# Graph quantile layer: 56 list gathers of the last pair as one-hot products on TensorE, and products and one-hot rows of the last batches on ACT

## The chip, the cores and the metric

The kernel runs on one core of a Trainium2 chip. The metric is device time in microseconds of one launch. Three runs of the kernel before gave 1544.91, 1548.63 and 1550.77 us; their median, 1548.63 us, is the time before. In this text PE is TensorE (PEld its weight load), DVE is VectorE, ACT is ScalarE, POOL is GpSimd and SP is SyncE. A tile is held as 128 partitions by some elements; a size such as 128x384 gives both.

## The reference

There are 16 graphs ("batches") of 1024 nodes with 64 channels each. The neighbours of a node are thinned by a rule on their rank; of each channel's values over the node and its remaining neighbours the quartiles are taken and added with weights 1/4, 1/2, 1/4; the sum goes through two dense layers. Cut to what matters:

```python
h = relu(layernorm(x))                                   # 16 x 1024 x 64
neigh = (adj > 0) & ~eye
nb = neigh.sum(-1);  rank = cumsum(neigh) - neigh
skip = where(nb > 10, (nb + 1) // 2, 1)
rem = neigh & (skip > 1) & (rank % skip == skip - 1) & mask
rem = rem | rem.T
nd = (adj > 0 or eye) and not rem                        # who counts for node n
s = sort(where(nd, h, inf), axis=neighbours);  nv = nd.sum()
for tau, w in ((.25, .25), (.5, .5), (.75, .25)):
    pos = tau * (nv - 1)
    agg += w * (s[floor(pos)] + frac(pos) * (s[ceil(pos)] - s[floor(pos)]))
out = x + (relu((h + agg) @ W1 + b1) @ W2 + b2) * mask
```

## The kernel before

The kernel has a list path, list_layer, which does all the work on this data, and a dense path behind a flag, which isn't entered here.

**Stages.** Batches go in pairs (m = 0 to 7, batches 2m and 2m+1). For each batch, prepare (L1629) loads the adjacency matrix, thins it (drop, keep), orders the 1024 nodes by their number of neighbours (order) and makes for each node a list of its neighbours' row numbers (collect, which ends with idx at L1132; lists[b] holds it). normalize writes the normalized rows of the batch to a table in DRAM. Then fetch (L1253) gathers, for each pair, the neighbours' rows of 64 f32 values: one indirect DMA of POOL (L1265) for each batch h, node tile k and list place s moves 128 rows. Nodes are ordered by list length, so the eight tiles of 128 nodes have lists of different lengths: FULL and HOSTS (L78, L79) set 12, 10, 9, 8, 8, 7, 5 and 4 gathers for tiles 0 to 7, 63 for each batch and 126 for a pair; the node's own row comes from an ACT copy (L1262). Eight pairs make the 1008 gathers of L1265. The 32 nodes with the longest lists are treated apart, for eight batches at a time ("the group", tile gg, with gathers of its own at L1531).

**Classes.** Tiles are sorted in four classes, (0), (1, 2, 3), (4, 5) and (6, 7), with 13, 11, 9 and 7 slots. The tile of a class is g0, g1, g4 or g6, with two buffers for g0 and g1 and one for g4 and g6 (bufs=2 - lo // 4): the next pair's gathers of tiles 4 to 7 wait until this pair has left them. sort (L1278) runs a fixed network of min and max over the slots of a class (L1297, L1300, L1305, on DVE), then multiplies the slots that can hold a quantile by their coefficients (L1316, on DVE, up to 384 elements an instruction) and lets PE add them into PSUM with an identity matrix (L1320). The order in which the slots are filled is in PLANS.

**Output.** After a pair's sums, ACT splits them into three bf16 terms (L1333), one_hot (L1414) makes rows that compare a running index with each node's number (L1418, DVE), and PE brings the sums back to the nodes' own order with them (sums, L1434 and L1440) and runs the two layers (mlp, L1448). For pairs 0 to 6 this follows the pair's sums; for the last pair the two halves and the two batches are interleaved by hand (aggregate with between, L1350 and L1650), so that batch 14's layers run beside batch 15's sort.

**Order.** The program is written as generators that yield costs. weave (L1602) runs results(m - 1) (sums and layers of the pair before) and beside it, in proportion, prepare for the next pair; and it issues the queued gathers bit by bit. In the loop at L1678, m = 7 has no batches left to prepare, so results(6) runs there with no side work, while the gathers of pair 7 are issued; m = 8 runs results(7). Afterwards arrange (L641) takes all instructions, works out who needs what, and sets each engine's order: it walks through time with costs of its own (cost, L614: 1330 ns for a gather, 55 ns + 0.87 ns an element and 75 ns a column operand for ACT, PE at its full clock) and at each moment gives an engine the ready instruction that stands first in the program. The engines then run in that fixed order. So a change in one place moves instructions elsewhere too. opened (L796) puts a very short memset (L799) behind a DVE instruction, and settle (L779) keeps a run of matmuls together with one semaphore at its end.

Of the kernel before, what the change touches and what calls it, by code (L numbers as in the profile page):

```python
# [31 lines left out]
F32 = mybir.dt.float32  # L32
F16 = mybir.dt.float16
BF16 = mybir.dt.bfloat16
# [30 lines left out]
CLASSES = (((0,), 13), ((1, 2, 3), 11), ((4, 5), 9), ((6, 7), 7))  # L65
# [19 lines left out]
FRONT = 134  # L85
# [667 lines left out]
def list_layer(  # L753
# [490 lines left out]
    def issue(many=None):  # L1244

        while queue and (many is None or many > 0):
# [3 lines left out]
            turn[0] += 1  # L1250
            many = None if many is None else many - 1

    def fetch(m, classes=CLASSES, halves=(0, 1)):  # L1253

        for tiles, slots in classes:
            lo, n = tiles[0], len(tiles)
            held, order = PLANS[slots][:2]

            def begin(h, tiles=tiles, lo=lo, n=n, slots=slots, held=held):
                if (m, tiles) not in gathered:  # L1260
                    gathered[m, tiles] = wk.tile([P, held, n, 2, C], F32, name=f"g{lo}", bufs=2 - lo // 4)
                nc.scalar.copy(gathered[m, tiles][:, slots - 1, :, h], owns[m][:, lo:lo + n, h])  # L1262

            def gather(h, slot, k, at, tiles=tiles, lo=lo):
                return nc.gpsimd.indirect_dma_start(  # L1265
                    out=gathered[m, tiles][:, slot, k - lo, h], out_offset=None, in_=tables[2 * m + h][0],
                    in_offset=bass.IndirectOffsetOnAxis(ap=lists[2 * m + h][:, at:at + 1], axis=0),
                    element_offset=tables[2 * m + h][1],
                )

            for h in halves:
                queue.append(partial(begin, h))
                for k in tiles:
                    for s, slot in enumerate(order[:FULL[k] + ((k, FULL[k]) in HOSTS)]):
                        queue.append(partial(gather, h, slot, k, PASSED[k] + s))


    def sort(lines, plan, first, coef, acc):  # L1278

        size = prod(lines.shape[2:])  # L1280

        def at(first, step, n):
            stop = first + step * (n - 1) + (1 if step >= 0 else -1)
            return lines[:, first:stop if stop >= 0 else None:step or 1]

        _, _, steps, ends, taken = plan
        most = max(1, PART // size)

        def parts(n):
            return [(k, min(most, n - k)) for k in range(0, n, most)]  # L1290

        for n, a, da, b, db, f, df, back, what in steps:
            run, others = [], []
# [13 lines left out]
            loose.update((then.ins.name, ins.ins.name) for ins, then in zip(run, others))  # L1307
            cost = (0.16 + n * size / 960) * (1 if f < 0 else 2)
            yield cost
        for n in taken:  # L1310
            now, ends = ends[:n], ends[n:]
            for k, many in parts(n):
                some = now[k:k + many]
                v = at(some[0], some[1] - some[0] if many > 1 else 0, many)
                v = v.rearrange("p s (k c) -> p s k c", c=C) if len(lines.shape) == 3 else v
                opened(nc.vector.tensor_tensor(  # L1316
                    v, v, coef(first + k, many)[:, :, :, None].to_broadcast(list(v.shape)), OP.mult
                ))
            settle([
                nc.tensor.matmul(  # L1320
                    acc, ident32, lines[:, s], start=False, stop=(s == now[-1] and not ends), skip_group_check=True
                )
                for s in now
            ])
            first += n
            cost = 0.16 + n * size / 960
            yield cost
# [22 lines left out]
    def aggregate(m, o, between=None):  # L1350
# [4 lines left out]
        for half in (0, 1) if last else (1, 0):  # L1355
            parts = CLASSES[2 * half:2 * half + 2][::1 if last else -1]
            for sides in ((0, 1), (1, 2)) if last and half else ((0, 2),):
# [56 lines left out]
    def one_hot(b, n, tag="at_p", bufs=1):  # L1414

        at = wk.tile([P, NT, HALF], BF16, name="at_p", tag=tag, bufs=bufs)
        for t in range(NT):
            opened(nc.vector.tensor_scalar(  # L1418
                at[:, t], iota[:, n * HALF:(n + 1) * HALF], node[:, b, t:t + 1], None, OP.is_equal
            ))  # L1420
            if t % 2:
                yield 0.6
        placed[b, n] = at
# [178 lines left out]
    def weave(main, total, side, side_total):  # L1602

        done = spent = 0.0
        turn[0] = 0
        for cost in main:
            done += cost / total
            issue(max(0, int(done * SPREAD) - turn[0]))
            while side is not None and spent / side_total < done:
                got = next(side, None)  # L1610
                if got is None:
                    side = None
                else:
                    spent += got
        for _ in side or ():
            pass
        issue()
# [89 lines left out]
def window(tiles, n):  # L1707

    return min(LEAST[k] for k in tiles) // 4, -(-3 * (n - 1) // 4) + 1
# [165 lines left out]
```

## Time and profile before

| | |
|---|---|
| Median of the runs | 1548.63 us |
| The profiled execution | 1547.62 us |
| Its span, first to last instruction | 1545.8 us |
| Mean granted PE clock | 0.840 |
| Last list ready (L1132, batch 15) | 1237.7 us |
| Last gather of pair 6 issued | about 1297 us |
| Last gather of pair 7 issued | 1487.5 us |
| Last sorting step | 1524.1 us |

"Busy" is the time in which an engine executes an instruction. An engine that isn't busy waits for data, for a buffer, or for its own issue. A group row gives the line, engine, operation and tiles, the count, the busy time in all and the mean of one in ns, then the idle time of the engine just before them and what ended it. A row of waits gives who waited for whom: us in total, how often, the longest. Matmuls of f32 count twice in the counts[...]. Instructions of DVE and ACT overlap their neighbours by a little, so the distance between two starts is shorter than the duration of one.

### The profile page before, as it was taken

What the parts mean: (1) busy time and instruction counts of PE and PEld (TensorE: products, weight loads), DVE (VectorE), ACT (ScalarE), POOL (GpSimd) and SP (SyncE); (2) the same over time, 40 slices, a digit from 0 to 9 for tenths busy, and PEclk for the clock granted to TensorE, in tenths of its full rate; (3) what the DMA queues carried; (4) which work ended last, traced back from release to release, by engine and by line L of the source; (5) the groups of instructions that cost most, each with busy time, mean ns of one, the idle gap of its engine ahead of it and who ended that gap; (6) DMA issues with size and microseconds to landing.
All of it is one profiled execution on the core that took longest, in us unless ns stands there. A gap on an engine that the chain in (4) does not pass through costs nothing.

```text
span 1545.8 us, 28097 instructions
## 1 busy us (share of the span) xinstructions
PE 1067.7 (69%) x8411; PEld 663.0 (43%) x8411; DVE 1249.8 (81%) x6125; ACT 915.4 (59%) x2504; POOL 1110.3 (72%) x1051
## 2 busy tenths in 40 slices
PE   6777867889886986798829964459867942450256
PEld 3444544555564544455516543335534521220223
DVE  5625389985899889978996798988998899689784
ACT  6998976989877884789557682186834410110001
POOL 3177775777777777777777777777777777777760
PEclk9979869899998998899869996769977975685567
DMA  6353432434433343335322342232311121121100
GB/s 213 103 178 87 118 93 78 114 86 122 96 111 86 88 126 83 87 76 129 85 66 79 67 133 50 45 100 59 93 34 28 26 53 24 30 52 24 25 15 16
DMA packets 128532, 122.85 MB, mean 79 GB/s; under 512 B 94546, under 2 KB 95090, under 8 KB 128370
## 3 DMA queue, kind: packets, MB, share of 16 engines
q1 hardware_dynamic: 95026, 86.77, 18.6%
q0 software_dynamic: 33344, 34.19, 12.0%
q8 instruction: 68, 1.11, 0.3%
q14 instruction: 94, 0.77, 0.2%
HBM read 110.10 MB, written 9.05 MB: 77 GB/s over the span
## 4 chain that ended last, share of the span: by engine, by line
ACT 28%; PE 23%; issue 18%; POOL 14%; DVE 10%; DMA 6%; DVEq 0%; SPq 0%; ACTq 0%; POOLq 0%
POOL g L1265 13%; PE codeP L1088 6%; ACT dist L991 5%; PE acc L1320 5%; ACT sg L904 4%; ACT ne L924 3%; ACT kept L1014 3%; DVE g L1300 2%; ACT waste L1186 2%; DMA at<-in_adj_dram 2%; DMA g<-gtab,idx 2%; DVE g L1305 2%; ACT waste L1181 2%; ACT xt L1194 2%; PE rk L981 1%
## 5 line engine op out<-in xcount | busy, mean ns | idle before, releaser
L1265 POOL DMA_INDIRECT g<-gtab,idx x1008 | 1055.0, 1047 | 367.7 <-issue 288.6
L1305 DVE TENSOR_TENSOR g<-g 128x384 f32<-128x384 f32 (+2 forms) x675 | 310.7, 481 | 6.4 <-DMA gg<-g 6.1
L1300 DVE TENSOR_TENSOR g<-g 128x384 f32<-128x384 f32 (+2 forms) x675 | 313.2, 484 | 1.5
L1320 PE MATMUL acc<-g,kf 128*128 128x128 f32 (+2 forms) x472 | 141.0, 448 | 159.9 <-DVE g L1316 106.6
L1088 PE MATMUL codeP<-pack,perm 128*128 128x332 bf16 x1024 | 184.9, 321 | 14.9 <-DVE perm L1063 14.5
L991 ACT ACTIVATE dist<-rk,bias 128x512 f16<-128x512 f32 x256 | 168.5, 708 | 31.2 <-DVE rem L992 19.9
L981 PE MATMUL rk<-kb,cnt 128*128 128x512 bf16 x256 | 112.5, 440 | 91.4 <-ACT dist L991 85.5
L1320 PEld LDWEIGHTS acc<-g,kf 128*128 128x128 f32 x472 | 90.1, 232 | 188.5 <-DVE g L1316 110.6
L911 PE MATMUL tp<-kb,sg 128*128 128x128 bf16 x1024 | 108.2, 242 | 71.6 <-ACT sg L904 50.2
L1014 ACT ACTIVATE kept<-kp 128x512 fp8e4<-128x512 f32 x248 | 146.8, 615 | 11.3 <-PE kp L1009 9.3
L924 ACT ACTIVATE ne<-tp 128x512 fp8e4<-128x512 f32 x248 | 141.5, 622 | 17.1 <-PE tp L917 9.7
L986 PEld LDWEIGHTS <-ne 128*128 128x128 fp8e4 x1024 | 89.9, 109 | 143.8 <-issue 120.9
L799 DVE MEMSET pause<- 128x1 bf16 x2340 | 138.1, 59 | 0.0
L904 ACT ACTIVATE sg<-at 128x1024 bf16<-128x1024 f32 x121 | 128.7, 1086 | 5.2 <-DMA at<-in_adj_dram 5.2
L1088 PEld LDWEIGHTS <-perm 128*128 128x128 bf16 x1024 | 93.4, 101 | 78.2 <-DVE perm L1063 37.8
L911 PEld LDWEIGHTS <-sg 128*128 128x128 bf16 x1024 | 80.6, 109 | 95.3 <-ACT sg L904 56.0
L986 PE MATMUL rk<-kw,ne 128*128 128x128 fp8e5 x1024 | 118.3, 241 | 0.0
L992 DVE TENSOR_SCALAR rem<-dist,half 128x1024 bf16<-128x1024 f16 x128 | 64.2, 503 | 52.2 <-ACT dist L991 51.4
L1009 PE MATMUL kp<-kw,rem 128*128 128x128 fp8e5 x1024 | 99.4, 218 | 0.0
L1004 PE MATMUL kp<-ne,kw 128*128 128x512 fp8e4 x256 | 97.2, 380 | 0.4 <-ACT dist L991 0.2
L1005 PE MATMUL kp<-rem,kw 128*128 128x512 bf16 x256 | 96.5, 377 | 0.0
L1418 DVE TENSOR_SCALAR at_p<-iota,node 128x512 bf16<-128x512 f16 x256 | 85.6, 376 | 11.8 <-PE low L1440 11.8
(189 smaller groups left out, 2071.5 us busy)
## 6 DMA issues: line engine op xcount, KB each, us to landing
at<-in_adj_dram SPq DMA_DIRECT2D x122, 512.0 KB
g<-gtab,idx POOLq DMA_INDIRECT x1008
xt<-in_x_dram SPq DMA_DIRECT2D x16, 256.0 KB
y<-in_x_dram SPq DMA_DIRECT2D x16, 256.0 KB
gtab<-xt SPq DMA_DIRECT2D x16, 256.0 KB
out_dram<-y SPq DMA_DIRECT2D x14, 256.0 KB
spare<-in_adj_dram SPq DMA_DIRECT2D x6, 512.0 KB
gg<-g SPq DMA_DIRECT2D x32, 48.0 KB
```

The costliest lines, as they stand in the source:

```text
L799: tails[nc.vector.memset(pause[:, at:at + 1], 0.0).ins.name] = ins.ins.name
L904: nc.scalar.activation(sg, at, AF.Sign)
L911: run.append(nc.tensor.matmul(tp[:, s], sg[:, m * P:(m + 1) * P], ident16, start=(s == 0), stop=(s == 3 and t // 4 != n), skip_group_check ...
L924: nc.scalar.activation(to, tp, AF.Relu, saturate=False)
L986: run.append(nc.tensor.matmul(rk[:, s * P:(s + 1) * P], ne[:, 4 * n + s, ts], upper, start=False, stop=(s == 3), skip_group_check=True,))
L991: nc.scalar.activation(dist[:, n * HALF:(n + 1) * HALF], rk, AF.Abs, bias=bias[:, t:t + 1])
L1014: nc.scalar.activation(kept[:, 4 * n:4 * n + 4], kp, AF.Relu, saturate=False)
L1088: run.append(nc.tensor.matmul(flat, perm[:, t, k * P:(k + 1) * P], pack[:, t], start=False, stop=(t == NT - 1), skip_group_check=True,))
L1265: return nc.gpsimd.indirect_dma_start(out=gathered[m, tiles][:, slot, k - lo, h], out_offset=None, in_=tables[2 * m + h][0], in_offset=bas ...
L1300: nc.vector.tensor_tensor(at(f + k * df, df, many), pa, pb, OP.min if what == "<" else OP.max)
L1305: nc.vector.tensor_tensor(pa if back else pb, pa, pb, OP.max if what == "<" else OP.min)
L1320: nc.tensor.matmul(acc, ident32, lines[:, s], start=False, stop=(s == now[-1] and not ends), skip_group_check=True)
```

## The change

Three things change, all in the last two pairs.

1. **Picks.** Of pair 7's gathers, the first LEAST[k] places of each list (LEAST = 8, 4, 4, 4, 4, 4, 0, 0 for tiles 0 to 7) are no longer issued to POOL: 28 for each batch, 56 in all. New functions do them. begin_pick reads the rows of batches 14 and 15 back from the table in DRAM, and splits each f32 into a bf16 half and two bytes in bf16 (three terms of 64 columns, exact). pick goes through the 56 in seven lots of eight. For each place, PE multiplies the broadcast index column by an identity matrix, so that the 128 row numbers stand along the free dimension on every partition; ACT copies them to f16 ("rows"); DVE compares them with the node number of each partition, for each of eight blocks of 128 nodes ("hot", 128x1024 an instruction, one buffer, in the place called "wide"); PE multiplies the one-hot blocks by the terms, 8 products of 192 columns a pick; ACT writes the result into the class tile, the bf16 half and the two bytes.
2. **Products on ACT.** For pairs 6 and 7 (ACTP = 6) the products by coefficients are done by ACT, one instruction of 64 elements with a scale column for each slot, tile and batch.
3. **One-hot rows on ACT.** For batches 14 and 15 (ACTB = 14) one_hot uses two ACT instructions for each DVE instruction: |index - node|, then relu(1 - that).

At m = 7 the picks are the side work of the weave: 20 steps of them are put ahead of results(6), the rest woven through it.

```diff
+ACTP, ACTB = 6, 14
...
+    def opening(some, m=B // 2 - 1):
+
+        tiles, slots = some
+        if (m, tiles) not in gathered:
+            gathered[m, tiles] = wk.tile(
+                [P, PLANS[slots][0], len(tiles), 2, C], F32, name=f"g{tiles[0]}", bufs=2 - tiles[0] // 4
+            )
...
                     for s, slot in enumerate(order[:FULL[k] + ((k, FULL[k]) in HOSTS)]):
-                        queue.append(partial(gather, h, slot, k, PASSED[k] + s))
+                        if m < pairs - 1 or s >= LEAST[k]:
+                            queue.append(partial(gather, h, slot, k, PASSED[k] + s))
+
+    def begin_pick():
...
+        nc.vector.tensor_scalar(first, first, float(FRONT), None, OP.add)
...
+            nc.sync.dma_start(
+                out=xt, in_=tab[at // C + FRONT:at // C + FRONT + N].rearrange("(t p) c -> p t c", p=P)
+            )
+            t = wk.tile([P, NT, 3 * C], BF16, name="terms", tag="at", bufs=2)
...
+            nc.scalar.copy(t[:, :, :C], halves[:, :, :, 1])
+            nc.scalar.copy(t[:, :, C:].rearrange("p t (c k) -> p t c k", k=2), bytes_[:, :, :, 0:2])
...
+    def pick(first, terms, index, wanted):
+
+        m = pairs - 1
+        for n in range(0, len(wanted), 8):
+            some = wanted[n:n + 8]
+            rows = wk.tile([P, len(some), P], F16, name="rows", tag="dist", bufs=2)
+            for at in range(0, len(some), 4):
+                tp = psum.tile([P, 4, P], F32, name="rowsT", tag="mx", bufs=3)
+                settle([
+                    nc.tensor.matmul(
+                        tp[:, q], index[h][:, PASSED[k] + s:PASSED[k] + s + 1].to_broadcast([P, P]), ident32,
+                        start=(q == 0), stop=(q == 3), skip_group_check=True,
+                    )
+                    for q, (h, k, s) in enumerate(some[at:at + 4])
+                ])
+                nc.scalar.copy(rows[:, at:at + 4], tp)
+            yield 0.5
+            hot = wk.tile([P, NT, 8, P], BF16, name="hot", tag="wide", bufs=1)
+            for j in range(NT):
+                opened(nc.vector.tensor_scalar(hot[:, j, :len(some)], rows, first[:, j:j + 1], None, OP.is_equal))
+                if j % 2:
+                    yield 1.0
+            for at in range(0, len(some), 2):
+                (h, k, s), (h2, k2, s2) = some[at:at + 2]
...
+                got = psum.tile([P, 2, 3 * C], F32, name="got", tag="code", bufs=2)
+                settle([
+                    nc.tensor.matmul(
+                        got[:, q], hot[:, j, at + q], terms[h][:, j], start=(j == 0 and q == 0),
+                        stop=(j == NT - 1 and q == 1), skip_group_check=True,
+                    )
+                    for q in range(2) for j in range(NT)
+                ])
...
+                nc.scalar.copy(halves[:, :, :, 1], got[:, :, :C])
+                nc.scalar.copy(bytes_[:, :, :, 0:2], got[:, :, C:].rearrange("p s (c k) -> p s c k", k=2))
+                yield 1.0
...
-    def sort(lines, plan, first, coef, acc):
+    def sort(lines, plan, first, coef, acc, by_act=False):
...
+                if by_act:
+                    w = coef(first + k, many)
+                    for i in range(many):
+                        for j in range(v.shape[2]):
+                            nc.scalar.activation(v[:, i, j], v[:, i, j], AF.Copy, scale=w[:, i, j:j + 1])
+                    continue
...
                         lines, plan, window(tiles, slots)[0], weigh, acc[:, lo - 4 * half:lo - 4 * half + n],
+                        m >= ACTP,
                     )
...
+            if b >= ACTB:
+                nc.scalar.activation(
+                    at[:, t], iota[:, n * HALF:(n + 1) * HALF], AF.Abs, bias=node[:, b, t:t + 1], scale=-1.0
+                )
+                nc.scalar.activation(at[:, t], at[:, t], AF.Relu, bias=ones_r[:, 0:1], scale=-1.0)
+            else:
+                opened(nc.vector.tensor_scalar(
+                    at[:, t], iota[:, n * HALF:(n + 1) * HALF], node[:, b, t:t + 1], None, OP.is_equal
+                ))
...
-        weave(chain(results(m - 1) if m else (), (1.0,)), 140.0 if m else 1.0, side, 85.0)
+        if m == pairs - 1:
+            side = pick(*begin_pick(), [
+                (h, k, s) for tiles, _ in CLASSES[:3] for h in range(2) for k in tiles for s in range(LEAST[k])
+            ])
+            for _ in range(20):
+                next(side)
+        weave(chain(results(m - 1) if m else (), (1.0,)), 140.0 if m else 1.0, side, 85.0 if m < pairs - 1 else 45.0)
```

More of the change, by code (lines that the diff above doesn't have):

```diff
@@ L1259, in begin @@
             def begin(h, tiles=tiles, lo=lo, n=n, slots=slots, held=held):
-                if (m, tiles) not in gathered:
-                    gathered[m, tiles] = wk.tile([P, held, n, 2, C], F32, name=f"g{lo}", bufs=2 - lo // 4)
+                opening((tiles, slots), m)
                 nc.scalar.copy(gathered[m, tiles][:, slots - 1, :, h], owns[m][:, lo:lo + n, h])
@@ L1274, in fetch @@
                     for s, slot in enumerate(order[:FULL[k] + ((k, FULL[k]) in HOSTS)]):
-                        queue.append(partial(gather, h, slot, k, PASSED[k] + s))
-    def sort(lines, plan, first, coef, acc):
+                        if m < pairs - 1 or s >= LEAST[k]:
+                            queue.append(partial(gather, h, slot, k, PASSED[k] + s))
+    def begin_pick():
+        first = wk.tile([P, NT], F32, name="first", bufs=1)
+        nc.vector.tensor_tensor(first, own2.rearrange("p (t k) -> p t k", k=2)[:, :, 0], own2.rearrange("p (t k) -> p t k", k=2)[:, :, 1], OP.add)
+        nc.vector.tensor_scalar(first, first, float(FRONT), None, OP.add)
+        terms, index = [], []
+        for h in range(2):
+            b = 2 * (pairs - 1) + h
+            xt = wk.tile([P, NT, C], F32, name="xt", bufs=1)
+            tab, at = tables[b]
+            nc.sync.dma_start(
+                out=xt, in_=tab[at // C + FRONT:at // C + FRONT + N].rearrange("(t p) c -> p t c", p=P)
+            )
+            t = wk.tile([P, NT, 3 * C], BF16, name="terms", tag="at", bufs=2)
+            halves, bytes_ = (
+                xt.rearrange("p t c -> p (t c)").bitcast(d).rearrange("p (t c k) -> p t c k", t=NT, c=C)
+                for d in (BF16, U8)
+            )
+            nc.scalar.copy(t[:, :, :C], halves[:, :, :, 1])
+            nc.scalar.copy(t[:, :, C:].rearrange("p t (c k) -> p t c k", k=2), bytes_[:, :, :, 0:2])
+            terms.append(t)
+            f = wk.tile([P, PASSED[-1]], F32, name="index", tag="keys", bufs=2)
+            nc.scalar.copy(f, lists[b])
+            index.append(f)
+        return first, terms, index
@@ new lines, in pick @@
+    def pick(first, terms, index, wanted):
[21 more added lines that the diff above has]
+                (h, k, s), (h2, k2, s2) = some[at:at + 2]
+                tiles, slots = next(c for c in CLASSES if k in c[0])
+                to = PLANS[slots][1][s:s + 2]
+                got = psum.tile([P, 2, 3 * C], F32, name="got", tag="code", bufs=2)
[6 more added lines that the diff above has]
+                ])
+                opening((tiles, slots))
+                step = to[1] - to[0]
+                end = to[1] + (1 if step > 0 else -1)
+                line = gathered[m, tiles][:, to[0]:end if end >= 0 else None:step, k - tiles[0], h]
+                halves, bytes_ = (line.bitcast(d).rearrange("p s (c k) -> p s c k", c=C) for d in (BF16, U8))
+                nc.scalar.copy(halves[:, :, :, 1], got[:, :, :C])
+                nc.scalar.copy(bytes_[:, :, :, 0:2], got[:, :, C:].rearrange("p s (c k) -> p s c k", k=2))
+                yield 1.0
@@ L1417, in one_hot @@
         for t in range(NT):
-            opened(nc.vector.tensor_scalar(
-                at[:, t], iota[:, n * HALF:(n + 1) * HALF], node[:, b, t:t + 1], None, OP.is_equal
-            ))
+            if b >= ACTB:
+                nc.scalar.activation(
+                    at[:, t], iota[:, n * HALF:(n + 1) * HALF], AF.Abs, bias=node[:, b, t:t + 1], scale=-1.0
+                )
+                nc.scalar.activation(at[:, t], at[:, t], AF.Relu, bias=ones_r[:, 0:1], scale=-1.0)
[3 more added lines that the diff above has]
+                ))
             if t % 2:
```

## The prediction

> **What bounds the kernel now.** I read four views in this order: the page's busy shares and chain, the waits of POOL and DVE after 1236 us, busy time by stretch there, and the rows of the operations that the change touches. 1236 us is where the last batch's lists are finished (idx, L1132, last at 1237.7 us); nothing that the change adds for batch 15 can start sooner.
>
> ```profile
> PE 1067.7 (69%) x8411; PEld 663.0 (43%) x8411; DVE 1249.8 (81%) x6125; ACT 915.4 (59%) x2504; POOL 1110.3 (72%) x1051
> L1265 POOL DMA_INDIRECT g<-gtab,idx x1008 | 1055.0, 1047 | 367.7 <-issue 288.6
> ```
>
> POOL looks less busy than DVE, but each gather of 1047 ns is followed by some 0.3 us of issue gap: 72% busy is a queue without a hole.
>
> ```profile
> POOL g L1265 <- issue: 50.3, 165, 0.3
> POOL g L1265 <- DMA g<-gtab,idx: 1.5, 5, 0.3
> ```
>
> These are POOL's waits from 1236 us on: no stall longer than 1.5 us until the last gather at 1487.5 us. So POOL is saturated to 58 us before the end. But DVE in the same stretches (columns: us, PE, PEld, DVE, ACT, POOL busy, PE clock, DMA share, GB/s):
>
> ```profile
> 1236.00:1256.00 20.00, 17.05 (x80) 8.91 (x78) 18.67 (x108) 6.61 (x17) 15.19 (x16) 1.00 0.27 53
> 1256.00:1337.00 81.00, 12.31 (x36) 7.65 (x37) 80.51 (x391) 0.59 (x2) 63.33 (x59) 0.55 0.17 33
> 1337.00:1376.00 39.00, 33.67 (x153) 19.18 (x152) 21.72 (x113) 12.02 (x24) 29.86 (x31) 0.93 0.21 46
> 1376.00:1433.00 57.00, 4.50 (x18) 4.12 (x19) 56.20 (x251) 0.00 (x0) 44.50 (x42) 0.50 0.15 29
> 1433.00:1444.00 11.00, 9.01 (x49) 7.92 (x47) 0.62 (x4) 1.27 (x4) 8.26 (x10) 0.78 0.15 26
> 1444.00:1524.00 80.00, 32.99 (x138) 18.30 (x138) 72.31 (x350) 7.49 (x19) 44.30 (x34) 0.67 0.10 18
> 1524.00:1546.00 22.00, 12.79 (x52) 7.15 (x52) 4.22 (x12) 3.67 (x7) 0.00 (x0) 0.66 0.06 16
> sum 310.00, PE 122.32 PEld 73.22 DVE 254.25 ACT 31.64 POOL 205.44; mean PE 17.47 PEld 10.46 DVE 36.32 ACT 4.52 POOL 29.35
> ```
>
> DVE is busy for 254.3 of these 310 us. Its idle time, stretch by stretch, is 1.3, 0.5, 17.3, 0.8, 10.4, 7.7 and 17.8 us. ACT is all but empty: 31.6 us of 310. What DVE waits for there:
>
> ```profile
> DVE yp L1508 <- PE yp L1504: 14.9, 6, 10.3
> DVE at_p L1418 <- PE low L1440: 7.1, 4, 5.7
> DVE highs L1461 <- PE low L1440: 7.0, 1, 7.0
> DVE g L1378 <- PE acc L1320: 6.6, 2, 3.7
> ```
>
> No line names a gather. The waits are the output layers of pair 6 and of the group, which the written-out order put where it had no sorting that it held ready. Gathers decide DVE's idle time only in this indirect way, through the order. So from 1236 us on there are two bounds close together, and DVE's is the harder: 254 us of work, of which the change takes little.
>
> **What the Trainium skill says.** *Perfetto Trace Analysis*, § Identifying the Most-Contended Engine: for Vector, Scalar and GPSIMD, occupancy is a fair measure of nearness to the limit. For DVE the trace agrees (80.51 of 81 us); for POOL it misleads, since the 0.3 us gaps are not counted. *VectorE: DVE Perf Modes*, § The perf-mode tier table: a tensor_scalar on 16-bit data in SBUF runs at 4x, an fp32 tensor_tensor at 1x. The trace agrees: 1024 16-bit elements take 478 ns at L1063, 384 fp32 ones 550 ns at L1305. *SBUF — State Buffer*, § Who interferes with whom: a DVE op in a two-port mode keeps GpSimd out of the shared ports. Gathers take 0.94 us where DVE idles (1433 to 1444 us) and 1.13 to 1.25 beside sorting; the added one-hot comparisons are of the locking kind. *ScalarE: Activation LUTs*, § What ACT_TABLE_LOAD costs: each [128,1] pointer operand adds about 93 ns and neighbours overlap by as much. L1186 (one pointer, 64 elements) takes 348 ns against 260 for L1181 without one, and its successor starts 0.25 us after it.
>
> **The change, part by part.**
>
> *Gathers removed.* Tiles 0 to 5 give up LEAST = 8, 4, 4, 4, 4, 4 slots in each of two batches: 56 of pair 7's 126. From 1349.5 to 1487.5 us POOL issues 102 gathers, 1.35 us each, so 56 are worth 76 us of POOL: its last gather would move from 1487.5 to about 1412 us. Pair 6's last 44 gathers, to 1297 us, remain.
>
> *One-hot rows added to DVE.* 56 picks in 7 lots of 8; each lot is 8 comparisons of 128x1024 f16 into bf16. Shape, types and operation are those of L1063, whose starts lie 0.41 us apart: 56 x 0.41 = 23 us. Bound: 27 us if nothing overlaps (0.478 each).
>
> *Products to ACT.* L1316 has 28 instructions of 384 elements (starts 0.48 us apart) and 14 of 256 (0.35) after 1236 us, exactly pairs 6 and 7: 13.4 + 4.9 = 18.3 us off DVE. ACT gets 112 instructions of 64 elements for each pair (slots x tiles x batches: 16 + 48 + 24 + 24), 224 in all, at 0.25 us (L1186's pitch): 56 us.
>
> *One-hot rows of batches 14 and 15 to ACT.* 32 instructions of L1418, 0.27 us apart: 8.7 us off DVE. ACT gets 64 of 512 elements with one pointer; L991, with one pointer and 512 elements from PSUM, has a pitch of about 0.58 us, so 37 us. Three quarters of these rows were fillers at 1237 to 1256 us; the first lots of picks can stand in their place.
>
> *ACT for the picks.* 14 copies of 128x512 (0.59 as L1333) 8.3 us; 28 pairs of copies out of PSUM, near L1097/L1098 but wider, about 0.7 a pair: 20 us; splitting two tables, as L1219 + L1220: 3.4 us, and two index copies. Sum for ACT: 31.6 + 56 + 37 + 32 = 157 us of some 290. It has room.
>
> *PE.* 56 x 8 products of 192 columns and 56 fp32 row broadcasts. L1088 takes 1.15 us for 8 x 332 columns at full clock, 0.43 ns a column; 192 columns are 0.083 us, or 0.16 at half clock. A lot is 64 of them, 5.3 to 10.6 us, plus 8 broadcasts at 0.25 to 0.5 us: 7 to 14 us. Over seven lots 50 to 100 us, where PE was busy 29 us of 101 (1236 to 1337). It fits beside the sort, barely at half clock.
>
> *SP.* Two table reads of 256 KB, under 4 us each as the xt rows of the chain; nothing waits for them but the picks.
>
> *The waits added.* The comparison tile has one buffer: lot n+1 on DVE waits for PE's last product of lot n, and behind it on DVE waits pair 6's sort. After the first 20 steps the lots are woven into pair 6's work, one for about a fifth of it, some 15 us of DVE; that covers 7 to 14 us of PE. The first three stand together, but beside the small work at 1237 to 1256 us. Nothing excludes a wait of 0 or of 10 us a lot; I take 4 us in all. Picks for tiles 4 and 5 wait for pair 6 to leave its buffer (about 1345 to 1356 us) and hold ACT's queue behind them, where the last copies of lots 5 and 6 are due anyway.
>
> *The end.* After the last sorting step DVE did two products of 0.48 us; now 12 of ACT stand there, 3 us, partly beside PE's sums: +1.5 us. Last step to end: 21.7 us before, 23 after.
>
> *Sum.* DVE work: +23 - 18.3 - 8.7 = -4. Waits on lots +4, end +1.5. What remains is the idle time before 1524 us, 38 us. With fewer gathers due, the order has class 0, the group and class 1 of pair 7 ready earlier to put into the 17.3, 10.4 and 7.7 us holes; I take that they shrink to 5, 2 and 6 (the chains of mlp through PE at half clock aren't known well to the order): -22.4. Sum -21 us: 1547.6 (profiled execution: span 1545.8 and 1.8 around it) becomes 1526.6. The median of the runs, 1548.6, lies 1.0 above it: 1527.6, forecast 1527.
>
> **The rivals.** *DVE's holes close entirely* (or POOL pays more): the floor is 1236 + 250.3 of DVE + 19.3 idle at the end = 1505.6, about 1508. The full 76 us, 1472, is shut out by DVE's work. For it: DVE is planned with everything ready. Against it: the mlp waits are on PE, not on gathers. *DVE-bound without gain*: the order keeps its holes, as the waits name PE and not POOL; then -4, +4, +1.5 leave 1541 to 1556, say 1549. For it: no DVE wait names a gather. Against it: the holes at 1340 to 1352 and 1433 to 1443 lie just where pair 7's gathers were outstanding in the queue. *Slower*: the single buffer of the comparison rows sets a round of DVE 3.3, PE 14 at half clock and ACT's last copy; if the order issues lots as soon as its own faster PE model has them free, DVE stands about 10 us a lot, 70 us in place of 4, while holes close as above: about 1527 + 45 (a third hidden) = 1572. It decides from 4 us a lot on (7 x 4 = 28, the gain and the 4 assumed). For it: PE ran at 0.55 of its clock at 1256 to 1337. Against it: 448 more products raise that clock, and the weave spreads the lots.
>
> **How the numbers follow.** Forecast (1515 to 1540) 0.52; holes close 0.14; no gain 0.18; slower 0.16. 0.5% or 7.7 us is what a measurement tells from no change: faster means under 1540.9. The first two cases make 0.66 faster, 0.18 the same, 0.16 slower. The range goes from the floor, 1505, to 1558, into the slower case, as a wait of up to 8 us on some lots would bring. The forecast's own range, 1515 to 1540, stands beside it.
>
> **What would show it.** Right: POOL's last gather near 1412 us; L1316's DVE work gone after 1236 us; comparisons at 0.41 us apart; DVE's holes at 1337 to 1376 and 1433 to 1444 small, DVE over 95% busy until 25 us before the end. Wrong: waits of the comparison rows on PE of over 4 us a lot, ACT's queue standing on a pick while products wait, or gathers still running late because class 1 or 2 waits for a buffer. If DVE waits name PE's output layers with 15 us and more, the "no gain" case is on.

## The result, and the profile after

Six runs of the changed kernel gave 1535.4 to 1537.97 us, with a median of 1536.15 us. Six runs of the kernel before on the same chip had a median of 1547.64 us. The ratio is 0.9924, with a 95% interval from 0.9912 to 0.9936: the change takes 11.5 us off, about half of the 21.6 us between 1548.6 and the forecast of 1527. The profiled execution took 1535.4 us, with a span of 1533.7 us and a granted PE clock of 0.867.

The page after, busy shares and the row of the gathers:

```profile
PE 1114.3 (73%) x8971; PEld 706.8 (46%) x8971; DVE 1241.5 (81%) x6091; ACT 1033.0 (67%) x2868; POOL 1034.0 (67%) x995
L1273 POOL DMA_INDIRECT g<-gtab,idx x952 | 986.8, 1037 | 351.7 <-issue 269.4
```

The 56 gathers are gone (952 in place of 1008), and ACT has 118 us more to do than before. DVE has 8.3 us less, over the whole run. POOL's waits from 1236 us on:

```profile
POOL out_dram L1688 <- DVE gx L1600: 75.4, 1, 75.4
POOL g L1273 <- issue: 30.5, 100, 0.3
```

The first row is new. POOL issues its last gather at 1402.57 us, 85 us earlier than before, and then stands for 75.4 us before the scatter of the group. The chain that ended last has no piece of POOL after 1388.3 us. The engines in the same stretches as before (columns: us, PE, PEld, DVE, ACT, POOL busy, PE clock, DMA share, GB/s):

```profile
1236.00:1256.00 20.00, 19.50 (x121) 11.92 (x120) 16.56 (x87) 14.15 (x35) 15.43 (x16) 1.00 0.26 52
1256.00:1337.00 81.00, 50.91 (x409) 41.01 (x406) 78.15 (x371) 34.56 (x125) 63.02 (x60) 0.79 0.17 34
1337.00:1376.00 39.00, 33.77 (x199) 22.56 (x200) 29.19 (x154) 21.00 (x70) 29.96 (x30) 0.87 0.13 27
1376.00:1433.00 57.00, 18.43 (x108) 12.55 (x107) 48.00 (x214) 30.30 (x63) 21.31 (x21) 0.65 0.15 32
1433.00:1444.00 11.00, 0.00 (x0) 0.00 (x0) 11.00 (x51) 0.00 (x0) 0.00 (x0) 0.50 0.00 0
1444.00:1524.00 80.00, 46.39 (x228) 28.94 (x228) 62.66 (x328) 34.07 (x122) 1.89 (x2) 0.79 0.02 5
1524.00:1546.00 22.00, 1.65 (x14) 1.43 (x13) 1.71 (x4) 0.49 (x1) 0.00 (x0) 0.85 0.06 16
sum 310.00, PE 170.65 PEld 118.41 DVE 247.26 ACT 134.56 POOL 131.61; mean PE 24.38 PEld 16.91 DVE 35.32 ACT 19.22 POOL 18.80
```

From 1236 us to the end DVE is busy for 247.3 of 297.7 us, where it was busy for 254.3 of 309.8. So 7.0 us of the 12.1 us between the two profiled spans are less work, and 5.1 us are less idle time. The hole at 1433 us is gone. In the place of the one at 1337 us there is one at 1362 to 1389 us that is nearly as large, but it isn't the same one. Most of the hole before lay at the end of pair 6's sums; these are DVE's waits there, in the kernel before (start, duration, engine, line, operation, tiles, then the idle time before it and its releaser):

```profile
1340.90 0.48 DVE L1378 MEMSET g<- 128x64 f32 x6 [3.72 <-PE acc L1320]
1344.23 0.19 DVE L1378 MEMSET g<- 128x64 f32 x2 [2.85 <-PE acc L1320]
1350.16 0.70 DVE L1418 TENSOR_SCALAR at_p<-iota,node 128x512 bf16<-128x512 f16 x2 [5.74 <-PE low L1440]
```

They are 12.3 of the 17.3 us. Behind them, from 1350.2 to 1376 us, pair 6's output layers ran with DVE busy for 20.8 of 25.8 us, since steps of pair 7's sort and a set of batch 14's one-hot rows stood between their instructions. After the change the end of the sums costs DVE 2.9 us (the last lot of picks stands there), and the output layers cost it 15.8. DVE's waits from 1236 us on, after:

```profile
DVE highs L1552 <- ACT highs L1551: 9.6, 2, 8.8
DVE yp L1599 <- PE yp L1595: 9.5, 7, 2.6
DVE yp L1599 <- ACT at_p L1504: 5.6, 1, 5.6
DVE at_p L1509 <- PE low L1531: 3.7, 5, 1.8
...
DVE hot L1331 <- PE got L1340: 2.9, 1, 2.9
DVE hot L1331 <- ACT rows L1327: 2.6, 1, 2.6
```

The last sorting step ends at 1511.2 us, and 22.5 us follow it. Of the 31 us that DVE idles between 1236 and 1511.2 us, 15.8 lie between 1362 and 1389.3 us, where it does nothing but the output layers of pair 6. This is how that hole begins and ends, in order of time on DVE (columns as above):

```profile
1361.78 0.56 DVE L1383 TENSOR_TENSOR gg<-gg 128x384 f32<-128x384 f32 x1
1364.11 0.84 DVE L1509 TENSOR_SCALAR at_p<-iota,node 128x512 bf16<-128x512 f16 x2 [1.77 <-PE low L1531]
...
1386.68 0.43 DVE L1599 TENSOR_TENSOR yp<-yp,mask 128x256 f32<-128x256 f32 x1 [5.57 <-ACT at_p L1504]
...
1389.30 0.56 DVE L1378 TENSOR_TENSOR gg<-gg 128x384 f32<-128x384 f32 x1 [0.27 <-PE gacc L1640]
```

The group's sort (gg) does four instructions, stops at 1362 us, and goes on at 1389.30 us, 0.27 us after gacc (L1640) on PE. That product adds the group's own rows, which a later step of the sort overwrites. Its accumulator has the PSUM tag agg, with two buffers, and the sums of pair 6's output layers (L1525, L1531) take both of them, one batch half after the other. The line with 5.57 us is a second matter. It is the chain of the last batch half through PE and ACT, and the row names ACT's one-hot rows as its end; h (L1572), the ACT copy in that chain, began at 1384.33 us, 0.7 us after its product, so the queue on ACT cost little. What was missing was something for DVE to do meanwhile.

The buffers are not the whole of it. ACT's copy of low (L1563), the last reader of the two buffers, ended at 1382.43 us, and gacc began 6.4 us later. In between it stood in PE's queue, behind the rest of the output layers and 40 products of the picks. These are the last 26 of them, and gacc:

```profile
1386.42 2.31 PE L1340 MATMUL got<-terms,hot 128*128 128x192 bf16 x26
1388.78 0.49 PE L1640 MATMUL gacc<-gg,kf 128*128 128x128 f32 x2
```

PE was busy for 27.07 of the 27.3 us, at a granted clock of 1.00. Some 9.9 us of DVE's idle time lie before 1382.4 us, and 5.9 behind it.

The chain that ended last, after (start, us, what):

```profile
1388.61 2.15 DMA g<-gtab,idx
...
1476.75 5.26 ACT g L1398 x22
...
1489.78 3.94 ACT g L1398 x16
...
1509.88 2.73 ACT g L1398 x11
```

The last gather on the chain landed near 1391 us. Before, the last one landed near 1456.5 us:

```profile
1453.77 2.73 DMA g<-gtab,idx
```

From 1473 us on the pieces of ACT's products on the chain add up to 15.2 us (0.96 + 0.97 + 0.95 + 5.26 + 3.94 + 0.37 + 2.73). They have become part of what sets the end.

### The profile page after: what moved, and what is told of

Same layout as the page of the kernel before. It is cut to its first block, busy times and chain, and to the rows that moved or that the text cites. A ratio compares the mean times of both kernels' runs of the same rounds, so it can differ in the third digit from the quotient of the medians.

```text
span 1533.7 us, 29482 instructions
## 1 busy us (share of the span) xinstructions
PE 1114.3 (73%) x8971; PEld 706.8 (46%) x8971; DVE 1241.5 (81%) x6091; ACT 1033.0 (67%) x2868; POOL 1034.0 (67%) x995
## 5 line engine op out<-in xcount | busy, mean ns | idle before, releaser
L1273 POOL DMA_INDIRECT g<-gtab,idx x952 | 986.8, 1037 | 351.7 <-issue 269.4
L992 ACT ACTIVATE dist<-rk,bias 128x512 f16<-128x512 f32 x256 | 167.6, 707 | 27.2 <-DVE rem L993 15.2
L1404 PEld LDWEIGHTS acc<-g,kf 128*128 128x128 f32 x472 | 86.6, 225 | 105.1 <-ACT g L1398 50.4
L1398 ACT ACTIVATE g<-g,coef 128x64 f32<-128x64 f32 x224 | 56.5, 337 | 87.9 <-DVE g L1378 64.3
L1094 ACT CAST st<-codeP 128x4 bf16<-128x4 f32 x128 | 21.0, 164 | 112.9 <-PE codeP L1089 112.8
```

What stands on the lines that cost most here:

```text
L992: nc.scalar.activation(dist[:, n * HALF:(n + 1) * HALF], rk, AF.Abs, bias=bias[:, t:t + 1])
L1273: return nc.gpsimd.indirect_dma_start(out=gathered[m, tiles][:, slot, k - lo, h], out_offset=None, in_=tables[2 * m + h][0], in_offset=bas ...
L1404: nc.tensor.matmul(acc, ident32, lines[:, s], start=False, stop=(s == now[-1] and not ends), skip_group_check=True)
```

## The experiments

Theory at the start: from 1236 us on DVE is the bound, and its work counts nearly one for one; POOL is a second bound close behind, which the picks take away for more than is needed. Rival 1: the removed gathers are the gain. Rival 2: the hole at 1362 to 1389 us, made by ACT's one-hot rows, ate the expected gain. A third rival came with the first experiment: only the work taken off DVE counts, and gathers never mattered.

The table gives the median, the ratio to the kernel before on the same chip, and from each profiled execution DVE's work over the whole run, its idle time (span less work), and the start of the last gather.

| | us | ratio (95%) | DVE work | DVE idle | last gather |
|---|---|---|---|---|---|
| before | 1547.6 | 1 | 1249.8 | 296.0 | 1487.5 |
| changed | 1536.15 | 0.9924 (0.9912 to 0.9936) | 1241.5 | 292.2 | 1402.6 |
| no picks | 1542.9 | 0.9965 (0.995 to 0.998) | 1223.5 | 324.3 | 1482.6 |
| picks only | 1554.6 | 1.0043 (1.003 to 1.0056) | 1268.9 | 286.4 | 1400.3 |
| one-hot rows on DVE | 1537.8 | 0.9931 (0.9907 to 0.9955) | 1249.8 | 288.9 | 1403.7 |
| products on DVE | 1556.7 | 1.0043 (1.0025 to 1.0062) | 1258.4 | 299.5 | 1405.0 |
| 40 picks | 1534.8 | 0.9916 (0.9899 to 0.9932) | 1233.1 | 300.6 | 1420.6 |
| 24 picks | 1528.8 | 0.9873 (0.9856 to 0.9889) | 1231.6 | 296.3 | 1444.1 |
| other PSUM buffers | 1531.65 | 0.9902 (0.9886 to 0.9919) | 1242.1 | 285.8 | 1404.4 |

The profiled executions of the first four experiments lie 2.4 to 6.6 us above their medians (6.6 for no picks), so their idle times are too high by about as much. The kernel before had a median of 1548.3 us beside the first four, and 1547.0 us beside the last three.

**No picks.** All gathers go back to POOL; ACT keeps its new work.

```diff
-                        if m < pairs - 1 or s >= LEAST[k]:
-                            queue.append(partial(gather, h, slot, k, PASSED[k] + s))
+                        queue.append(partial(gather, h, slot, k, PASSED[k] + s))
...
-        if m == pairs - 1:
+        if False:
             side = pick(*begin_pick(), [
...
-        weave(chain(results(m - 1) if m else (), (1.0,)), 140.0 if m else 1.0, side, 85.0 if m < pairs - 1 else 45.0)
+        weave(chain(results(m - 1) if m else (), (1.0,)), 140.0 if m else 1.0, side, 85.0)
```

> All 126 gathers of the last pair stay on POOL, no picks; ACT keeps the products of pairs 6 and 7 and the one-hot rows of batches 14 and 15. Theory (two bounds side by side, DVE the harder one from 1236 us on): DVE loses 27 us of work there, but POOL's last gather stays near 1487 us, so only what lies behind it gets shorter: 1538 to 1545 us, DVE with 20 us and more of new idle time that names gathers. Rival 1 (the removed gathers alone give the gain): 1545 to 1549, as before. Rival 3 (the gain is the work taken off DVE and nothing else, gathers never mattered): 1515 to 1525.

Measured: 1542.9 us, as the theory had it. Rival 3, 1515 to 1525, falls. DVE's work fell by 26.3 us (forecast for the two offloads: 27.0), and 28.3 us of idle time came in its place in the profiled execution; at the median it would be some 22, an estimate from the 6.6 us between the two times. In the two stretches where DVE had stood before, it stood again (39 us with 17.92 busy, 11 us with 3.90 busy):

```profile
1337.00:1376.00 39.00, 34.20 (x144) 18.73 (x146) 17.92 (x96) 19.59 (x51) 29.86 (x31) 0.87 0.17 40
1376.00:1433.00 57.00, 6.12 (x28) 4.97 (x28) 55.85 (x246) 12.59 (x29) 44.20 (x43) 0.54 0.15 33
1433.00:1444.00 11.00, 7.37 (x37) 7.16 (x38) 3.90 (x20) 0.34 (x2) 8.56 (x9) 0.58 0.13 28
```

That the new idle time would name gathers did not come true: no wait of DVE names one here either. That POOL still held the kernel, through the order, is so far an inference, from the distance between the last gather and the end: 58.3 us before (1545.8 - 1487.5) and 65.2 here (1547.8 - 1482.6). The run with 24 picks, below, is the test.

**Picks only.** ACTP and ACTB are set so that ACT gets nothing.

```diff
-ACTP, ACTB = 6, 14
+ACTP, ACTB = 99, 99
```

> The 56 picks replace gathers as in the changed kernel, but products and one-hot rows all stay on DVE. Theory (DVE is the bound from 1236 us on): DVE has 27 us more work than in the changed kernel, and the freed POOL buys nothing: 1555 to 1565 us, slower than the kernel before. Rival 1 (the removed gathers give the gain): 1534 to 1542 us, with DVE's holes filled by the added work.

Measured: 1554.6 us, slower than before, 0.4 us below the theory's range; rival 1 falls. POOL's last gather came at 1400.3 us, and that bought less than the picks cost: DVE's work rose by 19.1 us and its idle time fell by 9.6. Taken singly, the two halves are worth +6.3 us (picks) and -5.4 us (ACT), by their medians and 1548.3; together they are worth -11.5. The picks are worth 6.8 us once ACT has taken its part (1542.9 less 1536.15; 6.3 by the ratios).

**One-hot rows of batches 14 and 15 back on DVE.**

```diff
-ACTP, ACTB = 6, 14
+ACTP, ACTB = 6, 99
```

> The changed kernel with the one-hot rows of batches 14 and 15 back on DVE. Theory (DVE's work counts one for one): 8.7 us more of it, less the one wait of 5.6 us behind ACT's one-hot rows in pair 6's output layers: 1537 to 1545 us. Rival 2 (ACT's one-hot rows make the hole at 1362 to 1389 us that ate the gain): 1528 to 1535 us, with DVE's idle time there halved.

Measured: 1537.8 us; the intervals of the two ratios overlap. The wait of 5.57 us in the last batch half of pair 6 has become one of 1.74, as batch 14's one-hot rows now stand there on DVE; its work over the run is 8.3 us larger (forecast 8.7). The two nearly cancel, as they would if DVE did the rows in time that it would have idled. The difference of the ratios, 0.0007 with some 0.0027 to either side, leaves this part of the change between a loss of 3 and a gain of 5 us. Rival 2 falls as it was put: without ACT's rows the kernel isn't faster.

**Products back on DVE.**

```diff
-ACTP, ACTB = 6, 14
+ACTP, ACTB = 99, 14
```

> The changed kernel with the products of pairs 6 and 7 back on DVE. Theory (DVE's work counts one for one): 18.3 us more: 1549 to 1556 us. Rival 2 (ACT's longer queue holds up the output layers, so that its work is not free): 1536 to 1544 us, as the holes at 1362 to 1389 us and in the tail shrink.

Measured: 1556.7 us, 0.7 us above the theory's range, and 20.6 us more than the changed kernel (18.4 by the ratios), for 16.9 us of DVE work. The products are the part without which the change loses. Rival 2's form, that ACT's longer queue costs what it saves, falls too.

**Fewer picks.** PICK takes the place of LEAST where gathers are left out and picks listed; the steps put ahead and the weave's total follow the smaller number.

```diff
+PICK = (8, 4, 4, 4, 0, 0, 0, 0)
...
-                        if m < pairs - 1 or s >= LEAST[k]:
+                        if m < pairs - 1 or s >= PICK[k]:
...
-                (h, k, s) for tiles, _ in CLASSES[:3] for h in range(2) for k in tiles for s in range(LEAST[k])
+                (h, k, s) for tiles, _ in CLASSES[:3] for h in range(2) for k in tiles for s in range(PICK[k])
             ])
             for _ in range(20):
-                next(side)
+                next(side, None)
...
-        weave(chain(results(m - 1) if m else (), (1.0,)), 140.0 if m else 1.0, side, 85.0 if m < pairs - 1 else 45.0)
+        weave(chain(results(m - 1) if m else (), (1.0,)), 140.0 if m else 1.0, side, 85.0 if m < pairs - 1 else 26.0)
```

> The changed kernel with 40 picks, the slots of tiles 4 and 5 being gathered again. Theory (DVE's work counts, POOL has 75 us of slack at its end): 16 picks less are 16 x 0.41 = 6.6 us less of DVE, POOL's last gather comes at some 1424 us and nobody waits for it: 1528 to 1533 us. Rival 1 (each removed gather is worth time, since the order waits for gathers): 1537 to 1541 us.

Measured: 1534.8 us, between the two ranges, and by the ratios not to be told from the changed kernel (a difference of 0.0008, with some 0.002 to either side). DVE's work fell by 8.4 us, and its idle time rose by as much. With no picks for tiles 4 and 5, nothing stood any more in the gap at the end of pair 6's sums, where DVE now waited 8.0 us in one piece for the first one-hot rows' buffer. Work saved on DVE counted for nothing where it had been filling.

With PICK = (0, 4, 4, 4, 0, 0, 0, 0) and a total of 5.0:

> The changed kernel with 24 picks, those of tiles 1 to 3 alone. Theory (DVE's work counts, POOL has slack): 32 x 0.41 = 13 us less of DVE, last gather near 1446 us: 1522 to 1530 us. Rival 1 (each removed gather is worth time): more than halfway back to the run without picks (1542.9), 1538 to 1543 us.

Measured: 1528.8 us, ratio 0.9873 with an interval (0.9856 to 0.9889) wholly below the changed kernel's: this kernel beats both. DVE has 9.9 us less work than in the changed kernel (13 expected), 4.1 us more idle time, and POOL still waits at its end:

```profile
POOL out_dram L1689 <- DVE gx L1601: 13.7, 1, 13.7
```

With 32 gathers taken back, POOL's last one moved 41.5 us later (1402.6 to 1444.1), and the kernel became 7.4 us faster. So more than half of the picks freed an engine that nobody waited for. The time does not follow DVE's work step by step, though: from 40 picks to 24 the work fell by 1.5 us and the idle time by 4.3, and why this step alone brought 6 us isn't shown.

Against the run without picks, the 24 picks add 8.1 us to DVE's work, bring POOL's last gather from 1482.6 to 1444.1 us, and take 14.1 us off the time. With all gathers on POOL, then, the kernel was held up by them and the order that they force, though no wait names them; and 24 picks are enough to end that. The hole at 1337 to 1376 us, 17.3 us in the kernel before, stays here with 20 of 39 us:

```profile
1337.00:1376.00 39.00, 34.44 (x150) 19.17 (x150) 18.76 (x102) 19.50 (x51) 29.82 (x31) 0.88 0.19 40
```

**Other PSUM buffers.** 56 picks as in the changed kernel; the sums of batches 12 and 13 use mx and code in place of agg, so that the accumulators of the group and of pair 7 can begin earlier.

```diff
-                high, low = sums(o, placed.pop((b, n)), n, range(NT))
+                high, low = sums(o, placed.pop((b, n)), n, range(NT), late=b >= B - 4)
```

> The changed kernel, with the sums of batches 12 and 13 (pair 6's output layers) in the PSUM buffers of the tags mx and code in place of agg. Theory (the hole at 1362 to 1389 us is there because the group's and pair 7's accumulators wait for the two agg buffers, which these sums hold one after the other, and the sorts may not overwrite their own-row slot before it is added): sorting fills the hole, DVE's idle time there falls from 15.6 us to 5 or less: 1524 to 1530 us. Rival (the hole is there because nothing of pair 7 or the group is at hand, its gathers being outstanding): the idle time stays, 1534 to 1538 us.

Measured: 1531.65 us, 1.65 above the theory's range and below the rival's; the ratio is 0.9902, and its interval (0.9886 to 0.9919) just overlaps the changed kernel's; the difference of the two ratios, 0.0022 with some 0.002 to either side, is barely clear of zero. The mechanism shows in the trace. gacc's last product, at 1389.0 us in the changed kernel, is now at 1352.2 us (source view; the last two numbers are first and last start):

```profile
L1640 PE MATMUL gacc<-gg,kf x4: 272/275/378, 884.9 to 1352.2; 128*128 128x128 f32 x4
```

DVE in 1362 to 1389.3 us, first in the changed kernel, then with the other buffers (columns: us, DVE busy, PE clock, DMA share, GB/s):

```profile
1362.00:1389.30 27.30, 11.54 (x59) 1.00 0.25 51
```

```profile
1362.00:1389.30 27.30, 25.06 (x119) 1.00 0.22 45
```

The hole fell from 15.8 to 2.2 us. But a wait came up in front of it, while ACT multiplied the last slots of pair 6 and split its sums:

```profile
1364.10 0.86 DVE L1509 TENSOR_SCALAR at_p<-iota,node 128x512 bf16<-128x512 f16 x2 [9.46 <-PE low L1531]
```

In the changed kernel the last lot of picks stood in that gap, at 1355.8 to 1359 us; here it stands at 1383.5 to 1387.4 us, in the hole that was to be filled. So of the 13.6 us won in the hole, this wait takes a large part back, and the span is 5.8 us shorter. Without the two buffers' wait the hole closes, the part behind PE's queue with it, and its worth is about a third of its size.

**Combinations, on two other chips.** The last five runs (24 picks with the other buffers; no picks with them; 40 picks with them, twice; the kernel before with them) came to two chips on which the kernel before took 2741 and 2719 us.

> 24 picks (tiles 1 to 3), and the sums of batches 12 and 13 in the PSUM buffers of mx and code. Theory (DVE's work and the hole of the agg buffers are two separate costs): the 13 us less of DVE and the filled hole add up: 1520 to 1526 us. Rival (with 24 picks POOL's gathers are late again, so that nothing is at hand for the hole): as with 24 picks alone, 1527 to 1531 us.

> No picks, all gathers on POOL, ACT's products and one-hot rows, and the sums of batches 12 and 13 in mx and code. Theory (without picks POOL's last gather at some 1487 us sets the end): 1537 to 1544 us, as without picks and with the old buffers (1542.9). Rival (picks were never needed, the agg buffers alone made the holes): 1520 to 1530 us, DVE's idle time from 1236 us on below 45 us.

> 40 picks (tiles 0 to 3), and the sums of batches 12 and 13 in mx and code. Theory (costs add): 1534.8 less the 4.5 us that the same buffers gave with 56 picks: 1527 to 1532 us. Rival (tiles 0's picks are what fills the hole, so that it closes wholly here): 1518 to 1525 us.

> The kernel before, with nothing of the change, but the sums of batches 12 and 13 in mx and code. Theory (its hole at 1337 to 1376 us came from the agg buffers as well, but its end hangs on POOL's last gather at 1487 us): 1543 to 1548 us, little or no gain, with the idle time moved behind 1433 us. Rival (the buffers alone were before's loss): 1532 to 1540 us.

> 40 picks (tiles 0 to 3), and the sums of batches 12 and 13 in mx and code, once more, on a chip where the kernel before takes some 1548 us. Theory (DVE's work and the hole of the agg buffers are separate costs): 1534.8 (40 picks) less the 4.5 us of the other buffers: 1527 to 1533 us. Rival (class 0 and the group, ready early, close the hole wholly here, since DVE has fewer picks to do before it): 1518 to 1526 us, with DVE idle for less than 45 us from 1236 us on.

Measured: 2691.8 us, ratio 0.9813 (0.9784 to 0.9841), with 24 picks; 2733.6, 0.9961 (0.9946 to 0.9976), with none; 2660.2, 0.97 (0.968 to 0.9719), and on the second chip 2642.4, 0.9717 (0.9699 to 0.9735), with 40; 2741.9, 0.9996 (0.998 to 1.0011), for the kernel before with the other buffers. DVE's sorting steps last as long there as elsewhere (here is a row of the kernel before with the other buffers, 550 ns against 551); PE's granted clock was 0.685 in place of 0.840. Two of that kernel's waits:

```profile
L1300 DVE TENSOR_TENSOR g<-g 128x384 f32<-128x384 f32 x344 | 183.4, 550 | 18.7 <-issue 14.2 <-remote 3.4 <-PE acc L1364 0.3
```

```profile
POOL g L1265 <- PE acc L1320: 576.3, 10, 118.6
ACT dist L991 <- remote: 202.3, 18, 35.4
```

The engines stand for stretches of up to 55 us that the trace puts down to "remote" or "issue", that is, to nothing that it shows in the kernel, and POOL waits for the pair before. What made them isn't known. None of the expectations, which were made for 1548 us, can be decided by these runs. They only say that under such stalls more picks were better (none, 24, 40: 0.9961, 0.9813, 0.97), while the other buffers did nothing for the kernel before. Whether fewer picks and the other buffers add up at 1530 us stays open, and so does whether the other buffers would have done without picks.

## Why the prediction was right, and where its size was off

**Direction and bound.** Right. The forecast said that DVE, not POOL, is the harder bound from 1236 us on, and that the full 76 us of POOL can't be won. POOL's last gather was put near 1412 us and came at 1402.6; the time stayed 64 us above the 1472 that POOL's 76 us alone would have made. Five gathers more than before went out ahead of 1236 us, and the mean of those behind it, the group's included, was 1036 ns against 1061, so no slowing by the added comparisons shows. The reading behind that fear was too plain: beside sorting, at 1395 to 1433 us, the kernel before has gathers of 0.94 to 0.98 us as well as of 1.25. The runs without picks and with picks only show that neither half alone does it: POOL's gathers to 1482 us hold the one, DVE's work the other.

The time lies inside the forecast's range of 1515 to 1540, but nearer to the "no gain" case, which begins at 1541, than to the 1527 itself.

**DVE's work, forecast -4.** Measured -7.0 from 1236 us on (-5.9 of it up to the last sorting step) and -8.3 over the whole run. Products and one-hot rows came as priced: 16.9 and 8.3 us by the runs that put them back, against 18.3 and 8.7. ACT's copies of 64 elements did too: 16 in a row took 3.94 us, 0.25 each. The picks added 18.0 us to DVE's busy time where 23 were forecast (the changed kernel against the run without picks). The comparisons themselves were not cheaper: by the distances between starts in the trace, the 56 took 24.7 us, and it is the sorting steps of the changed kernel that took 6.1 us less than without picks. Why they did isn't shown. Nor is the 18.0 an even price: 16 picks made 8.4 us of difference between 56 and 40, and 1.5 between 40 and 24.

**Waits on the lots, forecast 4.** Measured 5.6 (2.9 + 2.6 in the two rows above, rounded). The rival of 10 us a lot didn't come: 448 products took 48.9 us on PE, 0.11 us each, inside the 0.083 to 0.16 assumed, and the lots were spread by the weave. PE's granted clock did rise with them: from 1256 to 1337 us it was 0.79 with PE busy for 50.9 us, where it had been 0.55 with 12.3.

**The end, forecast +1.5.** Measured +0.8 behind the last sorting step (22.5 against 21.7). But ACT's products stand on the chain in three places, 15.2 us in all; the forecast looked at the last of them alone, 3 us. DVE was busy 30.5 of the 36.6 us there, so that little of this shows as idle time.

**The holes, forecast -22.4: the term that failed.** The step said that holes of 17.3, 10.4 and 7.7 us "shrink to 5, 2 and 6" since class 0, the group and class 1 are at hand earlier. In the changed trace there are 15.8, 0 and 5.9 us. The second hole closed as forecast, and more. In the first, the end of pair 6's sums was filled, 12.3 us before and 2.9 after, but the output layers behind it, which had cost 5.0 us, now cost 15.8. Being at hand wasn't enough: the group's rows were there (its sort had begun at 1360 us), but the sort may not overwrite its own-row slot before PE has added it. That product waited until 1382.4 us for a PSUM buffer, and then for 6.4 us behind other products in PE's queue. The prediction read DVE's waits on PE's output layers and asked which data were missing; it didn't ask which buffers the output layers hold, nor what else would stand in PE's queue there. With other buffers the hole fell to 2.2 us, which is shown; that it would then have been worth its full size is not, as a wait of 9.5 us came in front.

Up to the last sorting step DVE was idle for 38.0 us before and is for 31.0 now, 5.6 of them waits on the lots. So the other idle time shrank by 12.6 us and not by 22.4. The measured terms, -5.9 of work, +5.6 on the lots, -12.6 of idle time and +0.8 at the end, make the -12.1 us between the spans.

**The sign of the "no gain" case.** The forecast named it: DVE's waits on PE's output layers at 15 us and more. Under PE's name they stand at 9.5 + 3.7 us, which is below that, and 5.6 more stand under ACT's name in the same layers, 18.8 in all. So by its letter the sign was not given, and by its meaning it was.

**What the forecast didn't ask** is how many picks are enough. It priced 56 gathers off POOL at 76 us and noted that DVE allows far less; the run with 24 picks shows that fewer were enough.

## What to carry to other kernels

When an engine is relieved at the cost of another, go only as far as the relieved one stops being waited for: here POOL ended with 75 us to spare, bought with DVE work, and giving 32 of 56 gathers back made the kernel 7.4 us faster. Where two bounds lie close together, test the halves of a change singly and together, since each half alone can look worthless or harmful. And before counting a hole as filled by work that is ready sooner, look for the buffers held across it (here two PSUM accumulators), for the in-place step that has to wait for them, and for the other work in the queue of the engine that makes the hole.

## What the runs showed of the hardware that was not expected

ACT's one-hot instructions from SBUF came some 0.68 us apart at 512 elements with a pointer operand, where a like one out of PSUM had suggested 0.58. DVE's comparisons of 1024 elements, 478 ns in the median, kept the same distance to what followed, whatever it was: none of the 56 is followed sooner than 0.405 us after its start, be it by another comparison or by a sorting step (one that starts at 1303.37 us has a sorting step behind it at 1303.78). A kernel's busy time on DVE can still grow by less than that, 18.0 us here for 56 of them, as the instructions around them change their distances too. So the price of an added instruction is better read from starts than from the busy totals of two kernels.
